# Combining the spectra at k and -k after the channel mixing instead of before it, in a fused convolution and feed-forward block

## The chip, the cores and the metric

The kernel runs on one core of a Trainium2 chip. The core has five engines that work at once, each through its own list of instructions in order: TensorE (PE, matrix products into PSUM), VectorE (DVE), ScalarE (ACT), GpSimd (POOL) and SyncE (SP, which here issues most of the DMA transfers). The metric is the device time of one execution in microseconds, median over runs.

## The reference, cut to what matters

The input `x` has 8 batches of 128 x 128 pixels with 96 channels. One layer of two residual blocks is computed:

```python
# block 1: a filter in the frequency domain, on the normalised input
x_pre = scale * relu(x @ w1.T) ** 2 + bias            # 96 -> 192 channels
xf    = rfft2(x_pre)                                   # 128 x 65 frequencies (k, l)
filt  = [resize(cw) for cw in (cw0, cw1, cw2)]         # 3 complex filters, 128 x 65 x 192
r     = softmax(small_mlp(means of x))                 # one rate per batch, filter and channel
y     = irfft2(xf * sum(r * filt)) @ w2.T              # 192 -> 96 channels
x     = x + y
# block 2: a feed-forward part with rounded arithmetic
t     = layernorm(x)
h     = relu(q_acc(q_acc(q_mul(t) @ q_mul(W1)) + q_mul(b1)))     # 96 -> 384
out   = x + q_acc(q_acc(q_mul(h) @ q_mul(W2)) + q_mul(b2))       # 384 -> 96
```

`q_mul` rounds to an 8-bit float (5 exponent bits, 2 mantissa bits), `q_acc` to a 16-bit float.

## The kernel before, in words

Each batch passes three streams, and a batch is in one stream while other batches are in others.

Stream **a** (`before`): 32 units of 4 image columns. The input is normalised, projected to 192 channels plus 48 context channels (`project`, PE, line 784), rectified and squared on ACT, transformed along the image height by one product with a matrix of cosines and sines (`transform`, line 813), folded on DVE (`fold`, 825) and stored to DRAM as Y. At its end a short chain (`rate_v0` to `rate_n`) makes the batch's filter rates.

Stream **s** (`spectrum`): 33 groups g. A group holds two frequencies k and k + 32 with their cosine and sine rows. `along_w` (PE, 997) transforms along the width; `filters_of` (PE, 1014) builds the filter values of the group from a table T, whose rows `weigh` (POOL, 987) has scaled by the rates; `copy_sr` (ACT, 1030), `make` (DVE, 1037) and `times` (DVE, 1043 and 1048) form the complex products at k and at -k. `turn_back` (POOL, 1059, twice a group) adds or subtracts the halves of these products into the tile `rr`. `real_basis` (POOL, 1072 and 1074) then adds and subtracts what belongs to k and to -k and writes `xf`, the real and imaginary part in the basis of cosines and sines. Two groups make one of 16 pairs p: `mix_low` and `mix` (PE, 1108) multiply `xf` by w2 into two PSUM banks `pv`, `mixed` (ACT, 1126) copies each bank, `invert` (PE, 1130) transforms back along the width with the matrix GL, `inverted` (ACT, 1135) copies, `store_v` stores to DRAM as V.

Stream **c** (`after`): 32 units of 4 columns in 8 blocks. `last` (PE, 1216) transforms back along the height, `residual` (DVE, 1222) adds x. After the normalisation `quantise` rounds to 8 bits (ACT, 1240; for every second column of the last batch `quantise_v` on DVE, 1238), `turn` (PE, 1245) transposes, `turned` (DVE, 1255) casts, `first` (PE, 1259) multiplies by W1, `accumulated` (ACT, 1266), `biased` (DVE, 1270) and `hidden` (ACT, 1274) round, add and rectify, `second` (PE, 1281) multiplies by W2, `put` (ACT, 1292) rounds, `bias` (DVE, 1296) adds the output bias for a block, `add_up` (POOL, 1299) adds the residual, and SP stores.

The table T is built once: `rows` (PE, 639) resizes the filters along the height, `row_put` copies and stores them, and `padding` (POOL and SP, 625 to 627) fills the unused of its 64 rows with zeros. The product `filters_of` uses 52 of the 64 rows.

The order is no loop order. Every step is entered in a list by `at(...)`, with the steps that it must follow. `in_order` then plans all engines ahead: it takes a cost per step from the table `COST`, and among the steps that an engine could begin soonest it takes the one with the lowest due time, from `WINDOWS` (start and length of each stream of each batch) and `OFFSETS` (per kind of step), with `WAIT`, `PATIENCE` and `TURN` as weights; `TURN` is added to PE's steps that would change the shape of its tiles (`QUARTER`: 64 x 64, other steps use the array whole). Six PSUM banks are handed out in this plan. The instructions are written in the planned order and pinned to it on each engine.

Of the kernel before, what the change touches and what calls it, by code (L numbers as in the profile page):

```python
# [43 lines left out]
MED = 192  # L44
# [24 lines left out]
    "a": ((-493.8, 43.6), (391.2, 548.2), (341.5, 669.9), (360.3, 112.8), (272.4, 474), (949.3, 682.8), (1532.2, 298.2), (2022.4, 291.1)),  # L69
    "s": ((419.4, 108), (361.2, 702.1), (621.3, 470.7), (1129.7, 501.9), (1112.5, 414.1), (1261.5, 485.3), (2142.2, 519.8), (1769.1, 212.4)),  # L70
    "c": ((643.4, 448.3), (913.9, 146.9), (1128.5, 301.3), (1948.4, 242), (1978.4, 471.2), (2323.9, 476.2), (2115.4, 99.6), (2601.6, 522.4)),
}
OFFSETS = {
    "a_context": -48.63,
    "a_fold": 49.78,
    "a_inverse": -197.71,
    "a_load_r": -12.98,
    "a_load_x": 18.54,
    "a_load_xT": -82.99,
    "a_measure": 28.7,  # L80
    "a_project": 54.76,
    "a_put": 22.3,
    "a_rate_e": -72.58,
    "a_rate_n": 307.71,
    "a_rate_p0": -87.61,
    "a_rate_p1": -45.78,
    "a_rate_p2": 8.73,
    "a_rate_v0": -246.94,
    "a_rate_v1": 95.58,
    "a_rate_v2": -255.23,  # L90
    "a_rate_v3": 112.84,
    "a_rectify": 7.95,
    "a_rest": 13.94,
    "a_root": -29.71,
    "a_scale": 65.86,
    "a_square": -3.1,
    "a_store_r": 47.62,
    "a_store_y": -73.43,
    "a_transform": -140.71,
    "a_variance": 57.57,  # L100
    "c_accumulated": -127.17,
    "c_add_up": -24.29,
    "c_bias": -7.57,
    "c_biased": -79.11,
    "c_first": -54.8,
    "c_hidden": 21.22,
    "c_inverse": 24,
    "c_last": -35.87,
    "c_load_v": -86.64,
    "c_measure": 192.55,  # L110
    "c_put8": 71.54,
    "c_quantise": 113.84,
    "c_quantise_v": 412.46,
    "c_residual": 7.8,
    "c_rest": -56.04,
    "c_root": 58.58,
    "c_second": -187.49,
    "c_store": 64.06,
    "c_turn8": -545.98,
    "c_turned8": 70.7,  # L120
    "c_variance": -102.78,
    "s_alone_t": 116.39,
    "s_alone_x": 156.62,
    "s_alone_z": 122.58,
    "s_along_w": -138.44,
    "s_copy_sr": -78.4,
    "s_filters_of": -23.17,
    "s_invert": -43.99,
    "s_inverted": -179.15,
    "s_load_t": 88.39,  # L130
    "s_load_y": 36.3,
    "s_make": 62.83,
    "s_mix": 40.57,
    "s_mix_low": -82.45,
    "s_mixed": -49.42,
    "s_real_basis": 33.95,
    "s_store_v": -18.14,
    "s_times": -182.14,
    "s_turn_back": 123.89,
    "s_weigh": -6.86,  # L140
}
WAIT, PATIENCE, TURN = (0.1, 0, 0, 0.06, 1.5), (16.9, 0.166, 10.6, 0.53, 42.4), 13.18
# [13 lines left out]
    "a_project": (PE, 0.975, 0),  # L156
    "a_transform": (PE, 0.809, 0),
# [20 lines left out]
    "s_real_basis": (POOL, 0.91, 0),  # L178
# [3 lines left out]
    "s_mixed": (ACT, 0.48, 0),  # L182
    "s_invert": (PE, 0.81, 0),
# [4 lines left out]
    "c_last": (PE, 0.809, 0),  # L188
# [5 lines left out]
    "c_turned8": (DVE, 0.68, 0),  # L194
# [6 lines left out]
    "c_bias": (DVE, 0.955, 0),  # L201
# [13 lines left out]
    "_padding": (POOL, 1, 2),  # L215
# [7 lines left out]
    "a_store_y": (ACT, 0.33, 1),  # L223
    "s_load_y": (SP, 3.2, 1.728),
    "s_load_t": (SP, 0.65, 0.576),
    "c_load_v": (SP, 2.1, 4.736),
    "s_store_v": (ACT, 0.33, 1),
# [5 lines left out]
SHARED = {"a_scale", "c_biased", "c_bias", "a_rate_n", "a_rate_v3"}  # L233
# [30 lines left out]
def _columns(p, r):  # L264

    if p < NP - 1:
        return [(g, cs) for g in (2 * p, 2 * p + 1) for cs in range(2)]
    return [(NG - 1, 0), (NG - 1, 1), (NG, r), (NG + 1, 0)]


def _constants():
# [22 lines left out]
    for p in range(NP):  # L294
        for r in range(2):
            for g, cs in _columns(p, r):
                k = g + 1 + 32 * r if g < NG else 32 if g == NG else 64 * r
                turned.append(k + 64 * cs)
# [3 lines left out]
        "GL": np.concatenate([weight * cos, -2 * sin[1:-1]]) * norm,  # L302
        "GK": np.concatenate([cos, -sin[1:-1]])[turned] * norm,
# [3 lines left out]
    rw = np.zeros((2, R, 2, L))  # L307
    sel = np.zeros((R, NS), np.float32)
    for s, (hh, ww) in enumerate(SCALE_HW):
        out[f"RH{s}"] = _resize_mat(hh, H)[order].T  # L310
        w = _resize_mat(ww, L).T
        for c in range(2):
            part = slice(c * NW + WOFF[s], c * NW + WOFF[s] + ww)
            for i in range(2):
                rw[i, part, c] = w * turn[0]
                rw[i, part, 1 - c] = w * turn[1] * (1 if c == 0 else -1)
            sel[part, s] = 1.0
    out["RW"], out["SEL"] = np.zeros((128, 2 * L)), np.zeros((128, NS))
    rw[1, :, 1] *= -1
    for i, p in enumerate((0, 64)):  # L320
        out["RW"][p : p + R], out["SEL"][p : p + R] = rw[i].reshape(R, 2 * L), sel
# [20 lines left out]
SAME = {"alone_z": "make", "alone_t": "times", "alone_x": "real_basis"}  # L342
# [27 lines left out]
def in_order(ops):  # L370
# [38 lines left out]
    while len(order) < n:  # L409
# [43 lines left out]
        if e == ACT and queued[i]:  # L453
            issue = t + 0.375
        else:
            last[e] = f
            if e == ACT:
                begun = t
# [31 lines left out]
def metaformer_kernel(ctx: ExitStack, tc: tile.TileContext, a: dict, out: bass.AP):  # L490
# [63 lines left out]
    GL = load(T_CONST, "GL", [128, 128])  # L554
    GK = load(T_CONST, "GK", [128, 128])
    W1q = const.tile([C, HID], F8, name="W1q")
# [5 lines left out]
    def projection(sp):  # L562
# [36 lines left out]
        def others():  # L599
            for i in range(2):  # L600
                nc.sync.dma_start(out=w2C[64 * i : 64 * i + 64, :, :], in_=a["w2T"].rearrange("(q m) c -> m q c", q=3))
            make_identity(nc, ident)
            nc.vector.tensor_copy(ident8, ident, saturate=False)
            nc.vector.memset(ones, 1.0 / (H * W))
            nc.vector.tensor_scalar(soa_bias, soa_bias, 128.0, None, ALU.mult)
# [6 lines left out]
    def filters(sp):  # L612

        zero = sp.tile([L, MED], F32, name="zero")

        rh = sp.tile([96, 128], F32, name="rh")
        cw = sp.tile([96, 2, max(ww for _, ww in SCALE_HW), MED], F32, name="cw")

        def load_scales():
            for s, (hh, ww) in enumerate(SCALE_HW):  # L620
                nc.sync.dma_start(out=rh[32 * s : 32 * s + hh, :], in_=a[f"RH{s}"])
                nc.sync.dma_start(out=cw[32 * s : 32 * s + hh, :, :ww, :], in_=a[f"cw{s}"])

        def padding():
            nc.gpsimd.memset(zero, 0.0)
            for s in range(2):
                nc.sync.dma_start(
                    out=T[s, R:, :, :].rearrange("r k m -> k r m"),
                    in_=zero.unsqueeze(1).to_broadcast([L, 64 - R, MED]),
                )  # L630


# [38 lines left out]
        at(T_ROWS[0] - 1, padding)  # L671
# [5 lines left out]
        for i in range(n):  # L677
# [3 lines left out]
            for k in puts:  # L681
                at(t + 1, row_put, i, k[3], after=[(None, "rows", i)])
        at(T_ROWS[1] + 5, weights, after=[(None, "row_put", n - 1, 2)])
# [272 lines left out]
    def spectrum(b, t0, P):  # L956

        stream[0] = "s", b
        pairs = ("mix", "mixed", "invert", "inverted", "store_v")
# [460 lines left out]
```

## Time and profile before

| | |
|---|---|
| median of 3 runs | 2857.3 us (2850.7 to 2861.2) |
| the profiled execution's own time | 2853.5 us |
| its span in the profile | 2851.7 us |
| PE busy | 2493.0 us (87%) |
| DVE busy | 2273.5 us (80%) |
| ACT busy | 2130.2 us (75%) |
| POOL busy | 2062.8 us (72%) |
| mean DMA rate | 218 GB/s |

A group in the profile is all instructions of one line with one shape: its busy time, the mean duration of one, and the idle time of the engine just before them with the instruction whose end finished it. PEld is the loading of weights into PE, which runs beside the products. Lines named L1059 and so on are those of the kernel before.

### The profile page before, as it was taken

The page shows a single profiled execution, that of the slowest core. Times are in us where ns is not written, and L with a number is a line of the kernel's source. Part 1 is how long each engine was busy: PE and PEld are TensorE (multiplying, and loading weights), DVE is VectorE, ACT ScalarE, POOL GpSimd, SP SyncE. Part 2 cuts the span into 40 slices and gives each one's busy share as a digit, 9 for nine tenths or more (in the row PEclk, how much of TensorE's full clock was granted, in tenths as well). Part 3 has the DMA queues.
Part 4 walks back from the last instruction along what each step waited for, and adds up shares of the span by engine and source line. Part 5 has one row for each costly group of instructions (what it writes and reads, how often), then busy time and mean ns, then how long its engine had stood idle before and what let it go on. Part 6 is the DMA issues. An engine that isn't in the chain of part 4 may idle for free. (4 is left out here: it accounts for less than half of the span.)

```text
span 2851.7 us, 98748 instructions
## 1 busy us (share of the span) xinstructions
PE 2493.0 (87%) x40122; PEld 1759.1 (62%) x40122; DVE 2273.5 (80%) x5110; ACT 2130.2 (75%) x4204; POOL 2062.8 (72%) x2983
## 2 busy tenths in 40 slices
PE   5788999899998999988989999999899888887775
PEld 3456666666766676766666666666667555665443
DVE  4567667887997899888878877897888987778785
ACT  2255544688886788978996577779799798787987
POOL 3136886777877887767888788798888787888433
PEclk9689998999999999989999999999999987989876
DMA  7688878988798898977669978785687663666431
GB/s 223 210 280 250 245 208 230 294 234 231 227 277 240 223 275 261 276 230 220 201 181 276 287 223 249 216 258 163 205 242 224 178 188 110 197 178 172 156 122 56
DMA packets 785657, 621.55 MB, mean 218 GB/s; under 512 B 578366, under 2 KB 719558, under 8 KB 785178
## 3 DMA queue, kind: packets, MB, share of 16 engines
q1 hardware_dynamic: 697138, 464.21, 58.9%
q10 hardware_dynamic: 88064, 151.02, 14.9%
q8 instruction: 316, 5.18, 0.8%
q14 instruction: 139, 1.14, 0.1%
HBM read 406.92 MB, written 208.16 MB: 216 GB/s over the span
## 5 line engine op out<-in xcount | busy, mean ns | idle before, releaser
L1059 POOL TENSOR_TENSOR rr<-t 128x390 f32<-128x390 f32 x512 | 500.6, 989 | 145.9 <-DVE t L1043 142.9
L784 PE MATMUL px<-W1S,zT 97*128 97x240 f32 x2048 | 513.8, 390 | 38.6 <-DVE yst L825 15.3
L784 PEld LDWEIGHTS px<-W1S,zT 97*128 97x128 f32 x2048 | 391.1, 199 | 137.9 <-DVE yst L825 23.8
L1266 ACT CAST y<-ph 128x512 f16<-128x512 f32 x768 | 410.9, 603 | 43.8 <-PE ph L1259 38.7
L813 PE MATMUL py<-X,F 128*128 128x384 f32 x1024 | 422.9, 530 | 16.4 <-ACT sr L1030 3.0
L795 ACT ACTIVATE rl<-px 128x480 f32<-128x480 f32 x512 | 289.9, 577 | 168.8 <-PE px L784 142.6
L1240 ACT ACTIVATE z<-t,ln_m,ln_r 128x96 fp8e5<-128x96 f32 x960 | 407.3, 476 | 10.8 <-DMA yt<-Yd 5.0
L1274 ACT ACTIVATE h<-y 128x1536 fp8e5<-128x1536 f16 x256 | 383.9, 1501 | 22.5 <-DVE y L1270 11.7
L1037 DVE TENSOR_TENSOR d<-pz,sr 128x390 f32<-128x390 f32 x512 | 265.7, 553 | 133.8 <-ACT sr L1030 132.6
L1270 DVE TENSOR_TENSOR y<-y,b1q 128x1536 f16<-128x1536 f16 x256 | 317.3, 1240 | 57.2 <-ACT y L1266 55.7
L1108 PE MATMUL pv<-w2C,xf 64*64 64x96 f32 x12288 | 319.9, 251 | 28.7 <-issue 24.0
L825 DVE TENSOR_TENSOR yst<-py,yb 128x384 f32<-128x384 f32 x512 | 261.8, 547 | 98.3 <-ACT yb L819 50.8
L809 POOL TENSOR_TENSOR sacc<-sacc,rl 128x192 f32<-128x192 f32 x248 | 167.7, 676 | 222.4 <-ACT rl L795 214.7
L1108 PEld LDWEIGHTS pv<-w2C,xf 64*64 64x64 f32 x12288 | 283.9, 138 | 71.6 <-issue 46.5
L987 POOL TENSOR_TENSOR tb<-tb,r 128x384 f32<-128x384 f32 (+1 forms) x264 | 302.0, 1145 | 27.2 <-DMA tb<-T 26.4
L1072 POOL TENSOR_TENSOR xf<-rr 128x390 f32<-128x390 f32 x256 | 291.3, 1138 | 13.6
L1043 DVE TENSOR_TENSOR t<-d,pf 128x780 f32<-128x780 f32 x256 | 245.2, 958 | 63.2 <-PE pf L1014 33.4
L1259 PE MATMUL ph<-zT,W1q 96*128 96x512 fp8e5 x768 | 258.4, 420 | 35.5 <-DVE zT L1255 20.0
L997 PEld LDWEIGHTS pz<-F,yt 64*64 64x64 f32 x12480 | 225.6, 138 | 93.6 <-issue 34.3
L997 PE MATMUL pz<-F,yt 64*64 64x65 f32 x12480 | 257.1, 226 | 20.6 <-issue 8.4
L1014 PE MATMUL pf<-RW,tb 52*64 52x130 f32 x6240 | 243.0, 283 | 31.7 <-POOL rr L1059 8.7
L1074 POOL TENSOR_TENSOR xf<-rr 128x378 f32<-128x378 f32 x256 | 266.9, 1043 | 0.0
(117 smaller groups left out, 4509.2 us busy)
## 6 DMA issues: line engine op xcount, KB each, us to landing
yt<-Yd SPq DMA_DIRECT2D x1040, 96.0 KB
Yd<-yst ACTq DMA_DIRECT2D x256, 384.0 KB
xb<-in_xw SPq DMA_DIRECT2D x64, 768.0 KB
zT<-in_xT SPq DMA_DIRECT2D x128, 384.0 KB
rB<-Rd SPq DMA_DIRECT2D x128, 384.0 KB
tb<-T SPq DMA_DIRECT2D x256, 192.0 KB
Vd<-gst ACTq DMA_DIRECT2D x128, 384.0 KB
t<-in_x SPq DMA_DIRECT2D x64, 768.0 KB
```

The lines of the kernel that those rows point to most:

```text
L784: nc.tensor.matmul(px[:, i * (MED + SCTX) : (i + 1) * (MED + SCTX)], lhsT=zTs[(b * NU // 2 + u // 2) % NZT][:, QW * (u % 2) + i0 + i, :], ...
L795: nc.scalar.activation(kept["rl", u][:, i0 : i0 + 2, :].rearrange("h w m -> h (w m)"), kept.pop(("px", u, i0)), AF.Relu)
L813: nc.tensor.matmul(py, lhsT=F1, rhs=kept["X", u][:, i0 : i0 + 2, :].rearrange("h w m -> h (w m)"), start=True, stop=True)
L987: nc.gpsimd.tensor_tensor(kept["tb", g][p, :], kept["tb", g][p, :], rates[b][p, :], ALU.mult)
L997: nc.tensor.matmul(halves[i][64 * k : 64 * k + 64, c * L : (c + 1) * L], lhsT=kept["yt", g][rows, cs, q, k, :], rhs=F2[rows, cs, :], start ...
L1059: nc.gpsimd.tensor_tensor(out, t[:, :, 0, :], t[:, :, 1, :], ALU.add if i else ALU.subtract)
L1072: nc.gpsimd.tensor_tensor(xf[:, :, :, 0:L], two(g, 0, 2, 0, L), two(g, 1, 2, 0, L), ALU.add)
L1108: nc.tensor.matmul(kept["pv", p, r][half, i * C : (i + 1) * C], lhsT=kept["xf", g][rows, cs, q, half], rhs=w2C[rows, q, :], start=(i == 0 ...
L1240: nc.scalar.activation(z, t, AF.Identity, bias=m, scale=r, saturate=False)
L1266: nc.scalar.copy(kept["y", u][:, n, :], kept.pop(("ph", u, n)))
L1270: nc.vector.tensor_tensor(y, y, b1q, ALU.add)
L1274: nc.scalar.activation(kept["h8", u], kept["y", u], AF.Relu, saturate=False)
```

## The change

`real_basis` is taken out. `turn_back` writes its two results straight into `xf`, so that `xf` holds what belongs to k and to -k side by side. The mixing, which is linear, is done on these (`_columns` puts the first kind in the first half of a bank and the second kind in the second half; for the sine rows of the second kind the weights are negated, `w2N`). Behind it `mixed` copies only the second half of a bank (192 columns instead of 384), and a new step `combine` on DVE adds the two halves into one V tile and subtracts them into another, reading the first half from PSUM. `invert` takes GL for the sums and a new matrix GM for the differences. At the ends l = 0 and l = 64 the two kinds cannot be told apart in this way; their filter values come from 12 extra rows of T, made once by `ends` and `end_put` from a second set of resizing matrices (RE). These take the place of the zeros, and `filters_of` uses all 64 rows.

The roundings are shared out anew in stream c: `turned` goes from DVE to ACT except in the last batch; every eighth column of `quantise` goes from ACT to DVE (in the last batch still every second one); `hidden` of the last batch is split, one third of it on DVE (`hidden_v`); `bias` goes from DVE to POOL. Buffers: `rr` goes; `B` and `V` have two tags of two buffers each. The two banks of a pair become free after `mixed` and both `combine` of each. All numbers in `WINDOWS` and `OFFSETS` differ, `WAIT` is 0 for all engines but SP's 1.42, `PATIENCE` and `TURN` (13.18 to 5100.78) differ.

```diff
-WAIT, PATIENCE, TURN = (0.1, 0, 0, 0.06, 1.5), (16.9, 0.166, 10.6, 0.53, 42.4), 13.18
+WAIT, PATIENCE, TURN = (0, 0, 0, 0, 1.42), (1.06, 54.4, 7.19, 78.2, 48.3), 5100.78
...
-    "c_bias": (DVE, 0.955, 0),
+    "c_bias": (POOL, 3.2, 0),
...
-SHARED = {"a_scale", "c_biased", "c_bias", "a_rate_n", "a_rate_v3"}
+SHARED = {"a_scale", "c_biased", "a_rate_n", "a_rate_v3"}
...
-        return [(g, cs) for g in (2 * p, 2 * p + 1) for cs in range(2)]
-    return [(NG - 1, 0), (NG - 1, 1), (NG, r), (NG + 1, 0)]
+        return [(2 * p + i, k) for k in range(2) for i in range(2)]
+    return [(NG - 1, 0), (NG, 0), (NG - 1, 1), (NG, 1), (NG + 1, 0)] if r == 0 else [(NG - 1, 0), (NG + 1, 0), (NG - 1, 1)]
...
+        "GM": np.concatenate([-cos[:1], -2 * sin[1:-1], -cos[L - 1 :], -2 * cos[1:-1]]) * norm,
...
+        def ends(s):
+            hh, ww = SCALE_HW[s]
+            p = slice(32 * s, 32 * s + hh)
+            for q in range(2):
+                pts["end", s, q] = pt = bank("pt")[:L, : 2 * MED]
+                for c in range(2):
+                    nc.tensor.matmul(
+                        pt, lhsT=re[p, 2 * q + c, :], rhs=cw[p, c, 0 : ww : ww - 1, :], start=(c == 0), stop=(c == 1)
+                    )
...
-                        p = slice(64 * s, 64 * s + R)
+                        p = slice(64 * s, 64 * s + 64)
...
+            x = kept["xf", g].rearrange("p s q n -> p (s q) n")
             if i == 0:
                 t = kept["t1", g].rearrange("p s (q c l) -> p (s q) c l", q=3, c=2)
+                nc.gpsimd.tensor_tensor(x[:, :, 0:L], t[:, :, 0, :], t[:, :, 1, :], ALU.subtract)
             else:
-                t = kept["t2", g]
-            out = kept["rr", g][:, 2 * i : 2 * i + 2].rearrange("p s q l -> p (s q) l")
-            nc.gpsimd.tensor_tensor(out, t[:, :, 0, :], t[:, :, 1, :], ALU.add if i else ALU.subtract)
-
-        def real_basis(g, i):
-            if ("xf", g) not in kept:
-                kept["xf", g] = psp.tile([128, 2, 3, 128], F32, name="xf", tag="xf", bufs=4)
-            xf = kept["xf", g]
-            if i == 0:
-                nc.gpsimd.tensor_tensor(xf[:, :, :, 0:L], two(g, 0, 2, 0, L), two(g, 1, 2, 0, L), ALU.add)
-            else:
-                nc.gpsimd.tensor_tensor(xf[:, :, :, L:], two(g, 2, -1, 1, L - 2), two(g, 3, -3, 1, L - 2), ALU.subtract)
+                t = kept["t2", g][:, :, :, 1 : L - 1]
+                nc.gpsimd.tensor_tensor(x[:, :, L:], t[:, :, 0, :], t[:, :, 1, :], ALU.add)
...
-                                rhs=w2C[rows, q, :],
+                                rhs=(w2N if k == 1 and h == 1 else w2C)[rows, q, :],
...
+            v = kept["B", p, r] = psp.tile([128, 2 * C], F32, name="B", tag=f"B{r}")
+            n = C if p == NP - 1 and r == 1 else 2 * C
+            nc.scalar.copy(v[:, :n], kept["pv", p, r][:, 2 * C : 2 * C + n])
...
+        def combine(p, r, cs):
+            if ("V", p, cs) not in kept:
+                kept["V", p, cs] = psp.tile([128, 2, 2 * C], F32, name="V", tag=f"V{cs}")
+            n = C if p == NP - 1 and r == 1 else 2 * C
+            v, a, b = kept["V", p, cs][:, r, :n], kept["pv", p, r][:, :n], kept["B", p, r][:, :n]
+            if cs == 0:
+                nc.vector.tensor_tensor(v, a, b, ALU.add)
+            else:
+                nc.vector.tensor_tensor(v, b, a, ALU.subtract)
...
-            xf = spectra(p) + [one("invert", p - 1, r) for r in range(2)]
+            xf = spectra(p) + [one("invert", p - 2, r) for r in range(2)] + [one("combine", p - 2, r, cs) for r in range(2) for cs in range(2)]
...
+            used = [[one("mixed", p, r), one("combine", p, r, 0), one("combine", p, r, 1)] for r in range(2)]
+            at(t, mix_low, p, after=xf, banks=2, until=used)
...
+        def quantiser(i):
+            return "quantise_v" if i % 8 == 7 or b == B - 1 and i % 2 == 1 else "quantise"
...
-            nc.vector.tensor_copy(kept["zT", u], kept.pop(("pz",) + divmod(u, NQ))[:C, :], saturate=False)
+            pz = kept.pop(("pz",) + divmod(u, NQ))[:C, :]
+            if b == B - 1:
+                nc.vector.tensor_copy(kept["zT", u], pz, saturate=False)
+            else:
+                nc.scalar.activation(kept["zT", u], pz, AF.Copy, saturate=False)
...
+            if n0:
+                nc.vector.tensor_scalar(h, y, 0.0, None, ALU.max, saturate=False)
+            else:
+                nc.scalar.activation(h, y, AF.Relu, saturate=False)
...
-            nc.vector.tensor_tensor(o, o, b2q.unsqueeze(1).to_broadcast([128, WB, C]), ALU.add)
+            nc.gpsimd.tensor_tensor(o, o, b2q.unsqueeze(1).to_broadcast([128, WB, C]), ALU.add)
```

## The prediction

> **What bounds the kernel now.** I read the table of stages first, because shares over the whole span average over unlike stages. I cut it where batch 0's filter rates are ready (227 us), where the last projected batch ends (2212) and where the last spectrum ends (2660). Columns: microseconds of the stage, busy time of PE, PEld, DVE, ACT, POOL, granted clock, DMA share, GB/s.
>
> ```profile
> 0.00:227.00 227.00, 163.97 (x502) 105.46 (x502) 128.19 (x461) 90.14 (x164) 66.23 (x196) 0.84 0.76 235
> 227.00:2212.00 1985.00, 1829.82 (x31197) 1318.45 (x31196) 1638.65 (x3617) 1510.64 (x3005) 1567.71 (x2202) 0.97 0.82 238
> 2212.00:2660.00 448.00, 374.29 (x7611) 261.40 (x7603) 366.87 (x714) 366.64 (x748) 367.61 (x472) 0.91 0.58 167
> 2660.00:2852.00 192.00, 124.90 (x821) 73.76 (x821) 139.82 (x322) 162.75 (x290) 61.27 (x114) 0.69 0.34 112
> ```
>
> Call them A, B, C, D. In A every engine waits. In B, 70% of the span, PE is busy 92% and the others 76 to 83%. In C (spectrum of batch 7 beside the feed-forward of batch 6) four engines stand level at 82 to 84%. In D (feed-forward of batch 7) ACT leads with 85%.
>
> Then the groups (line, engine, out<-in, count | busy, mean ns | idle before): the rows that the change touches.
>
> ```profile
> L1059 POOL TENSOR_TENSOR rr<-t 128x390 f32<-128x390 f32 x512 | 500.6, 989 | 145.9 <-DVE t L1043 142.9 <-DVE t L1048 2.5
> L1072 POOL TENSOR_TENSOR xf<-rr 128x390 f32<-128x390 f32 x256 | 291.3, 1138 | 13.6
> L1074 POOL TENSOR_TENSOR xf<-rr 128x378 f32<-128x378 f32 x256 | 266.9, 1043 | 0.0
> L1299 POOL TENSOR_TENSOR t<-t,o 128x1536 f32<-128x1536 f32 x64 | 205.3, 3208 | 75.2 <-DVE o L1296 75.2
> L1126 ACT COPY V<-pv 128x384 f32<-128x384 f32 x256 | 111.9, 486 | 125.2 <-PE pv L1108 119.1 <-DMA yt<-Yd 2.9 <-PE py L813 2.4
> L1255 DVE CAST zT<-pz 96x512 fp8e5<-96x512 f32 x256 | 172.8, 676 | 54.8 <-PE pz L1245 54.2
> L1296 DVE TENSOR_TENSOR o<-o,b2q 128x1536 f16<-128x1536 f16 x64 | 75.7, 1183 | 19.0 <-ACT o L1292 16.6 <-POOL xf L1074 2.1
> L1238 DVE TENSOR_SCALAR z<-t,ln_r,ln_m 128x96 fp8e5<-128x96 f32 x64 | 25.7, 450 | 0.5 <-POOL ln_m L729 0.5
> ```
>
> The reader should see that POOL spends 558 us on `real_basis` (L1072, L1074) and that L1072 had almost no idle time before it: POOL goes straight on from `turn_back`. Third, the waits, PE's own in stage B (engine, tile <- releaser: total us, times, longest):
>
> ```profile
> PE pv L1108 <- issue: 21.4, 15, 4.2
> PE pz L997 <- issue: 8.4, 9, 3.4
> PE pf L1014 <- POOL rr L1059: 8.3, 6, 3.6
> PE px L784 <- ACT sr L1030: 5.1, 3, 4.2
> ```
>
> Summed by releaser, PE's 149 us of waiting in B go to ACT 66, issue 38, DVE 23, POOL 17, DMA 5. POOL is nobody's last releaser for long; whatever it costs, it costs through others. Last, PE's timeline in a dense stretch (start, us):
>
> ```profile
> 1012.68 0.93 PE L997 MATMUL pz<-F,yt 64*64 64x65 f32 x48
> 1013.42 1.17 PE L1108 MATMUL pv<-w2C,xf 64*64 64x96 f32 x48
> ...
> 1019.38 0.93 PE L997 MATMUL pz<-F,yt 64*64 64x65 f32 x48
> 1020.24 1.56 PE L813 MATMUL py<-X,F 128*128 128x384 f32 x4
> ```
>
> 48 products `pz` take 0.74 us up to the next group in the same tile shape and 0.86 us up to one of another shape. A change of shape costs about 0.12 us, with no wait on record.
>
> **What the Trainium skill says.** "TensorEngine Tiling (Array Packing)", Key Properties: changing the tiling mode drains TensorE. The 0.74 against 0.86 us agree. "SBUF — State Buffer", SBUF: two separate sides: a VectorE instruction with two SBUF inputs or in a 2-port mode, and a GpSimd one, take the shared ports as an exclusive lock; the later blocks until the other is done. The trace agrees: `y` (L1270), two SBUF inputs, has 895 ns least, 984 median, 3746 longest, mean 1240; `z` on VectorE (L1238) 319 median, 3097 longest. "VectorE: DVE Perf Modes", Why PSUM operands drop a tier: a float32 operand in PSUM keeps VectorE at one element per cycle. The rows agree: 390 elements 553 ns, 192 elements (the copy `lg<-pl`) 345 ns.
>
> **The change, part by part.** Counts are from the built order of both kernels, durations from the rows.
>
> POOL: `real_basis` goes, -558. `turn_back` now writes `xf` itself, in blocks of 65 and 63 instead of one run. Its cost isn't shown; between L1059 (989) and L1072 (1138, blocked too). I take 1040: 512 x 0.05 = +26. The output bias (64 of 128x1536) comes to POOL; nearest row L1299, 3208 ns: +205. Sum -327: 2063 to about 1736.
>
> DVE: 496 `combine` of 192 columns and 16 of 96 come in, one operand in PSUM: 345 ns, +175. The cast L1255 leaves for 224 of 256: -151. The bias leaves: -76. 112 more roundings `z`: 319 ns unhindered, up to 760 if POOL blocks them as it does `y`: +36 to +85. 32 `hidden_v`: about +19. Sum +3 to +52; I take +25. The `combine` has one SBUF input, so no lock. The longer POOL instruction for the bias can hold a VectorE instruction for up to 3.2 us; the 512 vanished POOL instructions of about 1.1 us held it too. I count that as even.
>
> ACT: `mixed` halves, 486 to about 337 (the 195-column row `d<-pz`): -36. The cast moves in, 224 at the 603 of `y<-ph` (same 512 columns from PSUM): +135. 112 roundings less, 476 each: -53. `hidden` of batch 7, 32 x (1.50-1.06): -14. Sum +32.
>
> PE: as many `pv`, `pf`, `pz` products as before, `pf` over 64 rows instead of 52 (same 130 columns). Twelve extra products for the ends of l in stage A. Shape changes fall from 876 to 572 in the order: 304 x 0.11 = -33. DMA: the 1.2 MB of zeros at the start become as many bytes written around 100 us; the SP queue gets 14 more loads and stores, all in A. PE is idle 63 us of A, which covers most of the 14 us of extra products (12 at about 1.2 us, like `pt` there); s(0) waits for the rates, and if the covers failed A would grow by those 14. I take +3.
>
> The order shifts more than the sums. Adding up each stage's instructions, each by its row's busy time over its count (groups overlap, so sums run above busy time), I get before -> after:
>
> B: PE 2101 -> 2206, ACT 1676 -> 1790, DVE 1576 -> 1688, POOL 1605 -> 1384.
> C: PE 400 -> 312, ACT 420 -> 368, DVE 371 -> 279, POOL 376 -> 250.
> D: PE 115 -> 108, ACT 181 -> 155, DVE 162 -> 157, POOL 68 -> 94.
>
> So the new order does more of batches 4 to 7's later work inside B and leaves a thinner end. Stage by stage:
> B, at today's PE density: 1985 x 2206/2101 = 2084. Less 33 for shape changes. POOL falls from 81% to under 70% of the stage; between none and all of PE's 149 us idle could hang on it. I take a quarter, -35: **2016**.
> C: ACT leads, 420 of 448 = 94%. 368/0.94 = **391**.
> D: ACT 155/0.945 = 164, but DVE's 157 comes level and both POOL instructions of 3.2 us fall on it, and the last bias runs on POOL (3.2) not DVE (1.2) ahead of the last `add_up`: **182**.
> A: **230**. Sum 2819 of span. The profiled execution itself took 2853.5 for a span of 2851.7, and the median of the runs shown is 4 above it: +5, hence **2824**.
>
> Covers: the DVE's `combine` costs nothing only while PE has other work; it now stands between `mix` and `invert`. Both PSUM banks of a pair stay taken until two `combine` each are done, at least 0.7 us more; behind a `combine` on DVE stand `make` and `times` of the next group and the `residual` of stream c. Six banks serve all products, so PE pays if DVE is late.
>
> **The rivals.**
> *Nothing is gained, only shifted.* PE is at 92% in B; the trace names POOL for 17 of its 149 us. Then B is 2084-33 = 2051, the sum 2854, +5 = **2859**. Against it: C and D are thinner in any case.
> *POOL was the hidden pace-maker.* In C it is level with all others, and 143 us of waiting on DVE's `t` show it chained to the spectrum. If four fifths of PE's idle time goes, 119 us, B is 1932: **2740**. Against it: PE's direct waits.
> *Slower: DVE holds the PSUM banks.* In B DVE is 83% busy and takes 428 `combine` more; each waits behind instructions of 0.5 to 1.2 us with the banks held. If PE stands still 0.8 us on each of 107 pairs in B, that is +86, while the 35 from POOL don't come: **2945** at worst, 2902 with half of it. It decides once the stall exceeds about 0.3 us a pair (35 us). For it: DVE waits 216 us for ACT in B, and ACT now has the cast too. Against: PE waited only 23 us for DVE in B.
> That the change doesn't do what it says I exclude: the order shows `real_basis` gone.
>
> **How the numbers follow.** Forecast 0.42, hidden pace-maker 0.18, only shifted 0.15, slower through banks 0.25. Half a per cent (14 us) is about what this kernel's runs, 2850.7 to 2861.2, can tell from no change: 2843 to 2872 is the same. Faster: nearly all of the first two, 0.60; same 0.15; slower 0.25. The range leaves out the far ends of the pace-maker and of the bank stall: 2745 to 2895. The forecast's own is 2795 to 2850.
>
> **What would show it.** POOL about 1730 us, DVE 2280 to 2325, ACT 2160, PE 2450 to 2500. B near 2016 with PE at 93% or more; C below 400; D 175 to 190. The `combine` rows near 345 ns, the bias near 3200. The forecast fails if PE waits for DVE's V tiles, or ACT in stream c, by more than 35 us beyond today; or if the roundings on DVE take over 0.7 us each under POOL's new long instruction.

## The result, and the profile after

The changed kernel takes 2869.4 us (median of 9 runs, 2861.1 to 2888.5), the kernel before, run beside it, 2850.7 (2843.4 to 2866.2). The ratio is 1.0064, 95% interval 1.0037 to 1.0092: **slower by 0.6%**, where 2824 and faster was forecast. The profiled execution took 2874.9 us for a span of 2873.1.

The table of stages of the changed kernel, cut at the same events (rates of batch 0 ready, last projected batch, last spectrum). Columns as before: microseconds, busy time of PE, PEld, DVE, ACT, POOL, granted clock, DMA share, GB/s.

```profile
0.00:224.00 224.00, 165.79 (x513) 102.32 (x514) 129.17 (x464) 88.31 (x160) 61.11 (x193) 0.88 0.78 236
224.00:2335.00 2111.00, 1888.35 (x33002) 1412.64 (x33004) 1741.76 (x4105) 1616.13 (x3286) 1302.09 (x1935) 0.96 0.80 233
2335.00:2676.00 341.00, 278.97 (x5904) 201.77 (x5893) 278.57 (x586) 297.09 (x617) 240.16 (x291) 0.93 0.59 169
2676.00:2873.00 197.00, 117.37 (x760) 70.50 (x760) 155.78 (x333) 140.62 (x274) 92.94 (x116) 0.68 0.31 103
```

B is 2111 instead of the reckoned 2016; A, C and D together are 762 instead of 803. PE is busy 89% of B, less than the 92% of before.

The groups that answer to those shown before (line, engine, out<-in, count | busy, mean ns | idle before):

```profile
L1098 POOL TENSOR_TENSOR xf<-t 128x390 f32<-128x390 f32 x256 | 232.4, 908 | 348.7 <-DVE t L1084 337.2 <-PE pv L1136 7.0 <-PE px L825 2.2
L1101 POOL TENSOR_TENSOR xf<-t 128x378 f32<-128x378 f32 x256 | 247.9, 968 | 6.9 <-DVE t L1089 6.9
L1362 POOL TENSOR_TENSOR o<-o,b2q 128x1536 f16<-128x1536 f16 x64 | 202.4, 3163 | 95.2 <-ACT o L1358 95.1
L1169 DVE TENSOR_TENSOR V<-pv,B 128x192 f32<-128x192 f32 (+1 forms) x256 | 88.9, 347 | 110.1 <-ACT B L1155 98.8 <-ACT V L1161 10.9
L1295 DVE TENSOR_SCALAR z<-t,ln_r,ln_m 128x96 fp8e5<-128x96 f32 x176 | 115.9, 684 | 6.4 <-PE pz L1302 3.2 <-POOL ln_m L770 2.1 <-POOL tb L1028 0.9
L1316 ACT ACTIVATE zT<-pz 96x512 fp8e5<-96x512 f32 x224 | 135.8, 609 | 10.2 <-PE pz L1302 7.6 <-DMA yt<-Yd 1.1 <-PE pf L1055 0.7
```

POOL now waits 337 us for DVE ahead of `turn_back`, where it waited 143 before: it has been relieved. The new `combine` is as short as reckoned. Nothing in these rows is 95 us too long. The table of PE's own waits in stage B (tile <- releaser: total us, times, longest) has it:

```profile
PE pv L1136 <- issue: 63.4, 34, 4.1
PE pz L1038 <- issue: 22.8, 13, 3.5
PE pf L1055 <- issue: 20.6, 15, 4.2
PE pf L1055 <- POOL xf L1098: 13.3, 16, 2.0
```

"issue" is time in which PE waited for nothing that the profile shows. Summed by releaser, PE's idle time in B went from 149 us (ACT 66, issue 38, DVE 23, POOL 17, DMA 5) to 218 (**issue 120**, ACT 56, DVE 20, POOL 18, DMA 4): all but issue together fell from 111 to 98. Over the whole span PE is busy 43 us less and idle 65 us more (339 to 404), of which issue 43 to 134. Where such a wait falls is seen in PE's timeline of the changed kernel (start, us, instruction, count, idle before):

```profile
1022.55 0.93 PE L1038 MATMUL pz<-F,yt 64*64 64x65 f32 x48
1023.30 1.17 PE L1136 MATMUL pv<-w2C,xf 64*64 64x96 f32 x48
1024.30 0.88 PE L1038 MATMUL pz<-F,yt 64*64 64x65 f32 x48
1024.99 0.61 PE L1055 MATMUL pf<-RW,tb 64*64 64x130 f32 x13
1027.81 0.55 PE L1055 MATMUL pf<-RW,tb 64*64 64x130 f32 x10 [2.20 <-issue]
```

It comes in the middle of one step, after 157 records of small products in a row (a float32 product leaves two records, each with its weight load), and the products before and after the gap need nothing new. The page's table of DMA queues (packets, MB, share) lists instructions as transfers of their own:

```profile
q8 instruction: 317, 5.19, 0.7%
```

That is 16.4 KB a packet. PE has 40162 records and as many loads; if this queue is PE's, as the numbers suggest, a packet holds some 253 instructions, 127 records. The times of the packets in the trace say that it is: 75 of PE's 82 waits called issue, 124 of their 134 us, end 1.15 to 1.8 us after a packet of this queue has landed, a stretch in which only 7% of the span lies (in the kernel before 32 of 33). So "issue" is here a wait for instructions.

The profile also follows the chain of work that ended last, from the end back, at each step to what released it. In the changed kernel it can be followed back to 190 us, and it passes through 70 of the 82 waits, 118 of their 134 us. The gap above stands in it (start, us, what):

```profile
1025.17 0.43 PE pf L1055 x13
1025.61 2.20 issue
1027.81 0.52 PE pf L1055 x9
```

So most of these waits lie on the path that set the end. How close behind it another path lies, the chain doesn't tell; it is no measure of what their removal would bring.

In the built order of the kernel before, the longest run of 64 x 64 products between two whole-array steps is 216 records, and 9408 of some 31000 such records stand in runs of 144 or more. In the changed order the longest is 384, and 21564 stand in such runs: fewer shape changes (572 for 876) are the same thing as longer runs.

**Theory 1**: in long runs PE uses up its instructions faster than they arrive, and this costs the time. **Theory 2**: the supply stalls only fill time in which PE would have waited for something else; the 20 us come from another part of the change (the bias on POOL, banks held by `combine`, the plan).

### The profile page after: what moved, and what is told of

Read it like the earlier page. It is cut to its first block, busy times and chain, and to the rows that moved or that the text cites. A ratio compares the mean times of both kernels' runs of the same rounds, so it can differ in the third digit from the quotient of the medians.

```text
span 2873.1 us, 98792 instructions
## 1 busy us (share of the span) xinstructions
PE 2450.5 (85%) x40162; PEld 1787.2 (62%) x40162; DVE 2305.3 (80%) x5485; ACT 2142.1 (75%) x4332; POOL 1696.3 (59%) x2534
## 4 chain that ended last, share of the span: by engine, by line
PE 47%; ACT 17%; DVE 12%; issue 8%; DMA 5%; POOL 2%; SPq 1%; ACTq 1%; POOLq 0%; DVEq 0%
PE px L825 8%; PE pv L1136 7%; PE py L854 7%; PE pf L1055 5%; PE pz L1038 5%; ACT y L1327 5%; PE pg L1177 4%; ACT h L1340 4%; PE pk L1273 3%; PE po L1347 3%; PE ph L1320 3%; ACT z L1297 2%; DVE st L737 2%; DMA vin<-Vd 2%; DMA yt<-Yd 2%
## 5 line engine op out<-in xcount | busy, mean ns | idle before, releaser
L854 PE MATMUL py<-X,F 128*128 128x384 f32 x1024 | 446.1, 531 | 15.1 <-DVE yst L866 4.8
L1327 ACT CAST y<-ph 128x512 f16<-128x512 f32 x768 | 417.9, 603 | 45.1 <-PE ph L1320 35.7
L1098 POOL TENSOR_TENSOR xf<-t 128x390 f32<-128x390 f32 x256 | 232.4, 908 | 348.7 <-DVE t L1084 337.2
L1340 ACT ACTIVATE h<-y 128x1536 fp8e5<-128x1536 f16 (+1 forms) x256 | 371.6, 1452 | 22.1 <-DVE y L1331 20.8
L1297 ACT ACTIVATE z<-t,ln_m,ln_r 128x96 fp8e5<-128x96 f32 x848 | 363.0, 475 | 10.5 <-POOL ln_m L770 3.8
L1331 DVE TENSOR_TENSOR y<-y,b1q 128x1536 f16<-128x1536 f16 x256 | 308.3, 1205 | 77.8 <-ACT y L1327 77.1
L850 POOL TENSOR_TENSOR sacc<-sacc,rl 128x192 f32<-128x192 f32 x248 | 176.4, 711 | 303.3 <-ACT rl L836 290.8
L1055 PE MATMUL pf<-RW,tb 64*64 64x130 f32 x6240 | 253.5, 288 | 58.9 <-issue 24.9
L1055 PEld LDWEIGHTS pf<-RW,tb 64*64 64x64 f32 x6240 | 189.5, 139 | 130.0 <-issue 58.9
L1347 PE MATMUL po<-W2q,h 128*128 128x96 fp8e5 x3072 | 194.0, 218 | 81.3 <-ACT h L1340 54.3
```

The lines of the kernel that those rows point to most:

```text
L854: nc.tensor.matmul(py, lhsT=F1, rhs=kept["X", u][:, i0 : i0 + 2, :].rearrange("h w m -> h (w m)"), start=True, stop=True)
L1055: nc.tensor.matmul(pf[64 * k : 64 * k + 64, s, q * 2 * L : (q + 1) * 2 * L], lhsT=tb[p, m0 : m0 + 64], rhs=RW[p, :], start=True, stop=True,)
L1297: nc.scalar.activation(z, t, AF.Identity, bias=m, scale=r, saturate=False)
L1327: nc.scalar.copy(kept["y", u][:, n, :], kept.pop(("ph", u, n)))
L1331: nc.vector.tensor_tensor(y, y, b1q, ALU.add)
L1340: nc.scalar.activation(h, y, AF.Relu, saturate=False)
```

## The experiments

**The supply by itself.** A small kernel that leaves out the whole layer: runs of 24 to 256 small products, parted by 16 whole-array ones, first alone, then beside transfers of the input through SBUF to the output.

```python
for n in [24, 48, 64, 80, 96, 128, 192, 256]:
    small(n)      # 64 x 64 products of 65 columns, rows and columns of the array in turn
    rest(16)      # 128 x 128 products of 384 columns
```

> This kernel computes nothing of the layer: PE does runs of 24, 48, 64, 80, 96, 128, 192 and 256 small products (64 x 64 tiles, 65 columns, two records each, like the row pz), each run followed by 16 whole-array products of 384 columns; once with the DMA engines idle, once while x passes through SBUF to the output in pieces of 384 bytes. No instruction waits for another engine inside a run. Theory 1 (PE's instructions come in pieces of 16 KB, 256 instructions, and a piece takes longer than the 2 us in which small products use it up): short runs need 0.016 us a record, and from about 64 to 80 products (128 to 160 records) on PE stands still 1 to 4 us with nothing to wait for, again every 128 records; the run of 256 products takes 12 us or more instead of 8, more still beside the DMA load. Rival (the idle time called issue in the changed kernel is a wait that the profile misses, on VectorE's V tiles or a PSUM bank): all runs need the same time per record, about 0.016 us, with and without load.

Its timeline on PE, the longest run alone and then beside the transfers:

```profile
131.36 3.02 PE L37 MATMUL pq<-big 64*64 64x65 f32 x191
135.66 2.09 PE L37 MATMUL pq<-big 64*64 64x65 f32 x128 [1.28 <-issue]
139.12 2.09 PE L37 MATMUL pq<-big 64*64 64x65 f32 x128 [1.36 <-issue]
...
266.59 3.02 PE L37 MATMUL pq<-big 64*64 64x65 f32 x191
272.17 2.09 PE L37 MATMUL pq<-big 64*64 64x65 f32 x128 [2.55 <-issue]
276.17 2.09 PE L37 MATMUL pq<-big 64*64 64x65 f32 x128 [1.91 <-issue]
```

After 191 records PE stops, then after every 128: 128 records are used up in 2.1 us, and the next 128 start 3.46 us after the last. The packets of the queue in this trace show the loop: without the transfers, in the long runs, a packet begins about 1.1 us after PE has gone on with the one before, takes 0.9 to 1.4 us, and PE goes on 1.2 to 1.6 us after it has landed. Beside transfers the gaps are mostly longer, up to 3.2 us. Runs of up to 128 records, and those of 192, passed without a gap; in the other runs the first gap came after 159 to 255 records. So the supply is a limit of its own, in long runs one piece of 256 instructions about every 3.5 us, and no engine has to be late for it. That it costs the changed kernel its time is not shown by this.

**The planner's weights exchanged.** The changed kernel with PE's weights of before, and the kernel before with `WAIT` for PE at 0 as in the changed one.

```diff
-WAIT, PATIENCE, TURN = (0, 0, 0, 0, 1.42), (1.06, 54.4, 7.19, 78.2, 48.3), 5100.78
+WAIT, PATIENCE, TURN = (0.1, 0, 0, 0, 1.42), (16.9, 54.4, 7.19, 78.2, 48.3), 13.18
```

> The changed kernel, planned with the weights that the kernel before had for PE (WAIT 0.1, PATIENCE 16.9, TURN 13.18): PE changes its tile shape 858 times instead of 572, and runs of 144 or more small records hold 12384 records instead of 21564. Theory 1 (long runs of small products starve PE of instructions): PE's idle time called issue falls from 134 us to 50 to 70, PE's busy time grows by about 30, and the time falls to 2800 to 2835. Theory 2 (VectorE's combine holds the PSUM banks): issue stays above 110 us and the time stays within 0.5% of 2869. Theory 3 (only the shape changes count): 33 us more, about 2900.

```diff
-WAIT, PATIENCE, TURN = (0.1, 0, 0, 0.06, 1.5), (16.9, 0.166, 10.6, 0.53, 42.4), 13.18
+WAIT, PATIENCE, TURN = (0, 0, 0, 0.06, 1.5), (16.9, 0.166, 10.6, 0.53, 42.4), 13.18
```

> The kernel before, planned with WAIT 0 for PE as in the changed kernel: 630 shape changes instead of 876, runs of 144 or more small records hold 19332 records instead of 9408. Nothing else of the change is in it. Theory 1: issue grows from 43 us to 90 to 130, PE's busy time falls by about 25, the time rises to 2870 to 2910. Theory 2: issue stays near 43 us, the time falls by up to 25 us for fewer shape changes, 2825 to 2850.

The first took 2997.7 us, 1.051 of the kernel before (1.047 to 1.055): issue fell from 134 to 70, but PE's waits for ACT rose from 120 to 213, and PE's busy time by 68 us, with 858 shape changes instead of 572 and a granted clock of 0.922 instead of 0.932. The second took 2952.4 (1.036, 1.032 to 1.040): issue rose only from 43 to 64, waits for POOL from 32 to 71 and for ACT from 154 to 184. That is less issue than expected: this order has 19332 records in runs of 144 or more, nearly the 21564 of the changed kernel, and half its issue. So the length of the runs alone doesn't give the size of the stall. Neither decides between the theories: both plans got worse on the other engines, probably because windows and offsets belong to the weights.

**The output bias back on VectorE**, in the order of the changed kernel.

```diff
-            nc.gpsimd.tensor_tensor(o, o, b2q.unsqueeze(1).to_broadcast([128, WB, C]), ALU.add)
+            nc.vector.tensor_tensor(o, o, b2q.unsqueeze(1).to_broadcast([128, WB, C]), ALU.add)
```

> The changed kernel in its own order, with the output bias back on VectorE (64 instructions; POOL loses 202 us, VectorE gains about 70). Theory 1: the bias on POOL, 3.16 us each, blocks VectorE's roundings (684 ns instead of 319) mainly in the last stage; with it gone the last stage is 5 to 12 us shorter, the rest unchanged: 2855 to 2865. Rival (POOL's load still paces the middle): 20 us or more faster, below 2850. Rival (VectorE paces the middle): slower, above 2880.

2860.1 us, 1.0043 of before (1.0023 to 1.0062), against 1.0064 for the changed kernel: 6 us, and by the two intervals anything from nothing to about 16. DVE's busy time doesn't rise for its 64 extra instructions of 63 us in all (2305 to 2301), since others get shorter without this 3.2 us instruction on POOL: `z` falls from 684 to 561 ns (22 us in all), `y` from 1205 to 1140 (17 us). Issue stays at 130. The move of the bias can be a part of the 19 us, but with it undone the kernel is still slower than the kernel before.

**The long runs split.** Where a run would pass 144 records, up to two whole-array steps that the plan has ready are taken ahead; all else keeps its order.

```diff
+        if engine[i] == PE and quarter[i]:
+            here = RECORDS[kinds[i]]
+            if run + here > CAP:                       # CAP is 144
...                                                     # found: the next whole-array steps whose needs are met
+                    picked[at_i:at_i] = found
```

> The changed kernel in its own plan (same weights, same windows, same order of VectorE, ScalarE and SyncE to within single places), but wherever PE's run of 64 x 64 products would pass 144 records, up to two whole-array steps that are ready at that moment are taken ahead. 706 shape changes instead of 572, 12384 records in runs of 144 or more instead of 21564. Theory 1 (long runs starve PE's instruction supply): issue falls from 134 us to about 75, the changes cost 134 x 0.12 = 16, time 2825 (2805 to 2845). Theory 2 (the supply only fills time in which PE would have waited for something else, VectorE and the banks above all): issue falls likewise, other waits rise by as much, time 2870 to 2890.

> The split of e5_split together with the output bias on VectorE instead of POOL. Theory 1: the two gains add, 6 to 9 us below e5_split, about 2818; below the kernel before. Theory 2: like e5_split or above, 2865 to 2885.

2880.6 us (1.0115, 1.0066 to 1.0164), with the bias on VectorE 2875.2 (1.0097, 1.0066 to 1.0128). Issue fell to 102 us, where about 75 was expected, and PE's other waits rose by 37. By the numbers this is theory 2. But the split also moves PE's steps out of the places that the plan had found for them, so it changes two things at once.

**POOL's relief, put back and done alone.** In the changed kernel a further instruction behind each `turn_back`, which doubles the spectrum; in the kernel before `real_basis` emptied, which leaves out the combination of k and -k (`turn_back` writes into `xf`, which gets six buffers instead of four).

```diff
+            x = x[:, :, 0:L] if i == 0 else x[:, :, L:]
+            nc.gpsimd.tensor_tensor(x, x, x, ALU.add)
```

> The changed kernel in its own order with 512 more instructions on POOL, one behind each turn_back (xf = xf + xf in place, about 1.1 us each, +560 us, waited for by the mixing like real_basis before); it doubles the spectrum. It puts the relief of POOL back and nothing else. The forecast's term (a quarter of PE's idle time in stage B hung on POOL): +35, 2905. Rival, hidden pace-maker: +100 or more, 2970. Rival, only shifted: +15 at most, 2885.

```diff
         def real_basis(g, i):
-            ...
+            pass
```

> The kernel before in its own order with real_basis emptied: turn_back writes xf itself in blocks of 65 and 63, the mixing reads it as it is, so the combination of k and -k is left out. Runs of 64 x 64 products as before (max 216 records). POOL falls by about 540 us. The forecast's term: -35, 2815. Rival, hidden pace-maker: -100 or more, 2750. Rival, only shifted: 0 to -15, 2840. Theory 1 on the supply: issue stays at 40 to 55 us, since the runs are unchanged.

The load costs 79 us (2948.0; 1.034, 1.029 to 1.038). It delays every `xf`: PE waits 32 us for the new instruction ahead of the mixing. The relief alone brings 6 us (2844.2; 0.9971, 0.9950 to 0.9992), although POOL falls from 2063 to 1501 us and waits 341 us for DVE instead of 146. So in the order of the kernel before POOL paced almost nothing; the changed order suffers from a late `xf`, more than the forecast's 35 us.

**Both kernels planned anew with the supply in the plan.** The planner gets one rule: PE's instructions come in pieces of 256, each asked for when the one before is begun, there 3.9 us later (in the long runs of the small kernel PE went on after 3.5 us, beside the transfers after 4.0 to 4.8). Windows, offsets and weights were searched again, for the changed kernel with and without the rule.

```diff
+    took = [1.07 * t if e == PE else t for t, e in zip(took, engine)]
...
+            if done % PIECE == 0:                                  # PIECE is 256 instructions
+                stall = max(0.0, landed.get(k, asked.get(k, 0.0)) - at)
+                late, at = late + stall, at + stall
+                if k + 1 not in landed:
+                    asked[k + 1] = at + SUPPLY                     # SUPPLY is 3.9 us
```

> The changed kernel, instructions and buffers as they are, planned anew by its own planner with one rule more: PE's instructions come in pieces of 256, each asked for when the one before it is begun and there 3.9 us later; PE's costs times 1.07; windows and offsets searched for this rule. The plan ends at 2717.5 us. The order has 15456 records of 64 x 64 products in runs of 144 or more (21564 in the changed kernel). Kernels measured so far came out about 100 us above this plan's reckoning of them (101 the kernel before, 108 the changed one). Theory 1 (the supply starves PE and costs time): issue falls from 134 us to 30 to 60, time 2820 (2800 to 2845). Theory 2 (supply stalls only fill time in which PE would wait for something else): issue falls, other waits take its place, time 2855 to 2880.

> The same with the same search, but without the supply rule. Its plan ends at 2691 us, 26 earlier than that of e9_supply_plan; with the supply reckoned afterwards its order ends at 2754. 23208 records in runs of 144 or more. Theory 1: issue 100 to 140 us, time about 2855, some 35 above e9_supply_plan. Theory 2: 25 below e9_supply_plan.

> e9_supply_plan with the output bias on VectorE instead of POOL, order unchanged. If the bias on POOL costs what e4_bias_on_vector showed in the order of the changed kernel: 6 to 9 us below e9_supply_plan. If that gain hung on the old order: within 3 us of it.

> The kernel before, instructions and buffers as they are, planned anew with the same supply rule, the same factor on PE and the same search. Its plan ends at 2677 us; the order that it had ends at about 2750 by the same reckoning. 8424 records in runs of 144 or more, 832 shape changes. Theory 1, by the reckoning: time about 2780 (2760 to 2815), issue 15 to 40 us: then the kernel before, planned as well, is faster than the changed one. Rival (combining behind the mixing is worth its PE time and POOL relief once the supply is planned for): not below e9_supply_plan.

The changed kernel came out at 2938.8 us with the rule (1.030, 1.025 to 1.035), 2921.9 with the bias on VectorE besides (1.024, 1.019 to 1.030), and 2919.2 without the rule (1.023, 1.018 to 1.029). Issue behaved as the rule says, 74 with it and 112 without, but both plans were far above their reckoning, and PE waited more for ACT, POOL and DMA than in the changed kernel. Why the reckoning failed for them stays open. With the rule there is 38 us less issue and 20 us more time; if anything that speaks for theory 2, but again the work of all engines lies elsewhere. The kernel before, planned the same way, took **2806.0 us, 0.983 of its old time (0.979 to 0.988)**, and beats both kernels. Its issue waits are unchanged (46 us), so the gain isn't one of the supply. Most of it lies in PE's busy time (2493 to 2461, 1.3%), and the granted clock of its profiled execution is higher by as much (0.944, before 0.933). Why this order has a higher clock stays open.

**The same orders with fewer PE instructions.** This keeps each kernel's order and takes the supply out of play. Two 64 x 64 products that share rows become one of 64 x 128 in `along_w` and in the mixing, with the same result; in the changed kernel the negated weights become a sign that `mixed` applies.

```diff
-                    for k in range(2):
-                        for i in range(2):
+                    for i in range(2):
                             nc.tensor.matmul(
-                                halves[i][64 * k : 64 * k + 64, c * L : (c + 1) * L],
-                                lhsT=kept["yt", g][rows, cs, q, k, :],
+                                halves[i][:, c * L : (c + 1) * L],
+                                lhsT=kept["yt", g][rows, cs, q].rearrange("w k m -> w (k m)"),
...
-            nc.scalar.copy(v[:, :n], kept["pv", p, r][:, 2 * C : 2 * C + n])
+            nc.scalar.activation(v[:, :n], kept["pv", p, r][:, 2 * C : 2 * C + n], AF.Copy, scale=sign)
```

> The changed kernel in its own order, with two products 64 x 64 that share their rows made one of 64 x 128, for along_w (k = 0 and 1 side by side) and for the mixing (both halves of l; the sign of w2N is applied by mixed as a scale per partition). filters_of stays 64 x 64. PE issues 16321 products instead of 22513, 3096 records in runs of 144 or more instead of 21564; 255 more shape changes, +28 if each costs what the others do. What a product of 64 x 128 takes is not known and is the same in e14_before_wide. Theory 1 (starved supply costs time): issue falls from 134 us below 40, and the changed kernel gains about 45 more than the kernel before does by the same edit: e13 some 25 us below e14. Theory 2 (the stalls only fill other waiting): issue falls as well, both kernels gain or lose alike, e13 some 20 above e14.

> The kernel before in its own order with the same edit (along_w and the mixing in products of 64 x 128). 16301 products instead of 22493, none in a run of 144 records or more; 198 more shape changes. Issue falls from 43 us below 25 under both theories. If a 64 x 128 product takes up to twice a 64 x 64 one: time 2830 to 2870.

> The order of e12_before_supply_plan (2806 us) with the same edit as in e14_before_wide. It should differ from e12_before_supply_plan by as much as e14_before_wide does from the kernel before, within 15 us.

The changed kernel with this edit took 2936.0 us (1.032 of before, 1.028 to 1.035), the kernel before with it 2999.8 (1.055, 1.052 to 1.058), its newly planned order 2942.7 (1.034, 1.032 to 1.036). The edit is a loss everywhere: a product of 64 x 128 does the work of two of 64 x 64 and takes over three times as long as one. The groups of `along_w` and of the mixing in the changed kernel with the edit; the first has 6240 records at 423 us busy, where 12480 took 257:

```profile
L1038 PE MATMUL pz<-F,yt 64*128 64x65 f32 x6240 | 423.0, 281 | 8.9 <-ACT rl L837 3.8 <-ACT y L1326 1.4 <-DMA yt<-Yd 1.4
L1135 PE MATMUL pv<-w2C,xf 64*128 64x96 f32 x6144 | 408.2, 284 | 0.0
```

But it hits both kernels alike (PE's busy time rises by 252 and by 258 us), and with it **issue is gone from both**: 134 to 4 us in the changed kernel, 43 to 0 in the kernel before. Of the waits of the changed kernel this one is left:

```profile
PE pf L1055 <- issue: 3.7, 3, 3.0
```

The busy time of the engines, share of the span and instructions, in the changed kernel and then in the kernel before, both with the edit:

```profile
PE 2702.0 (91%) x27778; PEld 2040.2 (69%) x27778; DVE 2321.3 (79%) x5486; ACT 2184.3 (74%) x4332; POOL 1685.1 (57%) x2534
PE 2750.8 (92%) x27738; PEld 2026.1 (68%) x27738; DVE 2258.0 (75%) x5110; ACT 2154.2 (72%) x4204; POOL 2042.7 (68%) x2983
```

And now the changed kernel is 64 us faster than the kernel before, ratio 0.978 (about 0.974 to 0.982, from the two ratios and their intervals), where without the edit it is 19 slower. The swing of 83 us stands beside a difference of 90 us between their issue waits. The profiled executions, whose granted clocks are nearly equal (0.937 and 0.936), show less, since that of the changed kernel was its slowest of five: their spans are 2956.6 and 3001.1 us, a lead of 44.5 us where there had been a lag of 21.4, so a swing of 66. PE's idle time is 237 and 232 us in them, where it had been 404 and 339. By this estimate some 60 of the 90 us of issue were idle time on top, and the rest stood in the place of other waits.

The newly planned order of the kernel before is a control. Its issue waits are like those of the old order (46 and 43 us), and the edit costs it 137 us, the old order 149: where the supply doesn't differ, the edit moved the difference by 12 us. It also shows a limit. With the edit this order and the changed kernel are level (2942.7 and 2936.0 us), so the 64 us are a lead over one order of the kernel before, not over all that its instructions allow.

This speaks against theory 2: in the same orders, with the same banks, bias and combination, the disadvantage goes when the stalls go. It doesn't exclude it. PE is busy 91 to 92% of the span here, so that what the change saves on PE (49 us between the two) counts in full, and 250 us more of PE's work leave all other engines more time: what the banks, the bias or the plan cost in the tighter schedule may vanish together with the stalls. The edit also puts 57 more new shape changes on the changed kernel than on the other (255 and 198), which makes its lead smaller and not larger.

Taken together: it is shown that the added idle time of PE is a wait for instructions, and that these waits lie on the path that set the end. That they turn a gain of some tens of microseconds into a loss of 19 is what the last experiment says, but the split and the new plan of the changed kernel, which took a part of the stalls away in other ways, brought no time. So the supply is the likely cause and not a proven one, and what each stall costs in the unedited order stays open.

## Why the prediction was wrong

**The step that failed** is the one for B: "B, at today's PE density: 1985 x 2206/2101 = 2084. Less 33 for shape changes." The busy part of it holds: PE's 1830 us in B times 1.05, less 33, is 1889, and 1888 was measured. What fails is that idle time stays in proportion. The 304 vanished shape changes were entered as a gain alone. They are the same runs grown longer, and issue in B, 38 us x 1.05 = 40 by the density, measured 120: +80. I had read "issue: 21.4, 15, 4.2" in the first line of PE's waits and taken it as a fixed cost of the engine. The count of long runs in the built order would have warned that it could grow, though not by how much: the kernel before planned with `WAIT` at 0 has nearly as many and 64 us of issue in all.

**The second term of B**, a quarter of PE's idle time for POOL's relief (-35): all of PE's other waits in B are 98 us, where 111 x 1.05 = 117 would have stood without relief. So -19 instead of -35, and the relief done alone in the kernel before gave 6 us. The two errors make 80 + 16 = 96; B was 95 above the forecast.

**C and D.** C was 341 against 391 and D 197 against 182, together 35 us less than forecast. Why C is 50 us shorter isn't followed here; without this luck the miss in B would have shown in full, and not as 54 us of the span. In D I had named that both long POOL instructions fall on DVE, and sized it too small: `z` takes 580 ns there (450 before), and PE waits for DVE 37 us instead of 14.

**The parts.** POOL 1696 (about 1736): `turn_back` costs 908 and 968 ns, not 1040. DVE 2305 (2280 to 2325), ACT 2142 (2160), PE 2450 (2450 to 2500), the combination 347 and 338 ns (345), the copy of B 325 (337), the cast on ACT 609 (603), the bias 3163 (3208), `z` on DVE 684 (319 to 760). A came out at 224 (230). Every sum of work came within 2.5%. Of the marks "PE at 93% or more" in B failed, at 89%, and D, at 197 us where 175 to 190 was named. Two slips of reading carry no sum: the 48 records of a step of `along_w` are 24 products of two records each, and POOL's share of B before is 79% by the table of stages (81% is the sum of rows).

**The rivals.** *DVE holds the banks* has the right sign and not the mechanism: PE waits for DVE 20 us in B, less than before. *Only shifted* is nearest in time, 2859, but it too kept PE's density. *POOL the hidden pace-maker* falls with the relief done alone. None of them had the wait that came; it stood in the first line of the table that I quoted.

## What to carry to other kernels

Count how many instructions an engine uses up per microsecond in its densest stretch, not only how long they take: in the small kernel PE used 256 instructions in 2.1 us and got them every 3.5, and a change that only groups small products closer together made it wait. A saving in shape changes has to be set against the length of the runs that it makes, and an "issue" line among an engine's waits deserves a look at what stands before each of its gaps. To test a suspected limit, take it away from both kernels with their orders kept; moving work out of its way in a planned order changes all other waits as well.

## What the runs showed of the hardware

PE's instructions arrive in packets of 16.4 KB, some 256 instructions, and in a long run of small products no faster than one in about 3.46 us, longer beside other transfers (gaps of up to 3.2 us instead of 1.4). These packets are not fetched ahead there: without the transfers each begins about 1.1 us after PE has gone on with the one before. Float32 records of 64 x 64 start in fours, 7 ns apart within a four, a four every 58 ns at 65 columns and every 83 ns at 96 (the kernel before). Records of 64 x 128 start in pairs, 7 ns apart, a pair every 112 ns at 65 and at 96 columns alike (the kernel before with the edit). "TensorEngine Tiling (Array Packing)" in the Trainium skill, Key Properties, says that tiles execute in parallel; in both shapes the trace agrees. What makes a pair last 112 ns isn't the number of streamed columns, which doesn't change it; it may be the loading of weights of 128 columns instead of 64, which no run here tests.
